# A third Strassen level in five rounds of a two-level product, with loads and small work reordered

## Chip, cores and metric

The kernel runs on one core of a Trainium2 chip. The metric is the device time of that core in microseconds, as a median of three runs. Everything is float32.

The engines named below are TensorE (PE), VectorE (DVE), ScalarE (ACT), GpSimd (POOL) and SyncE (SP), which issues nearly all large transfers.

## The reference

x has the shape 32 x 128 x 2048. It is mixed along its channels with kernels that depend on a condition, passed through a large linear layer with low-rank updates, and added to itself. Then a grouped convolution and a permuted, grouped two-layer network follow, again with a residual.

```python
att = softmax(mlp(cond))                                   # 32 x 8
agg_w = einsum('bk,koi->boi', att, weight)                 # 32 x 128 x 128
h = einsum('boi,bih->boh', agg_w, x) + (att @ bias_k)[:, :, None]
x = x + h @ W.T + bias + sum_e w_e * (h @ A_e.T) @ Bf_e.T  # W: 2048 x 2048, 16 experts
y = conv1d(x, weight9, groups=4) + cond @ c_weight.T + bias
y = y[..., perm] as 16 heads of 128
x = x + unperm(gelu(y @ up_h) @ down_h)                    # 128 -> 512 -> 128
```

The low-rank updates are folded into W ahead of time, and the mixing along channels is applied after the linear layer. So the largest part of the first half is one product of x (all rows, 2048 wide) with a 2048 x 2048 matrix. The change is within that product.

## The kernel before

**Rounds and steps.** The product is cut into 2 x 2 blocks by Strassen-Winograd: seven products of blocks in place of eight. These are the seven rounds, in the order P1, P2, P6, P7, P5, P3, P4 (`ROUNDS`, L48). In each round the weight operand stays and x runs past it in eight steps g = 0 to 7. Step number i is 8 x round + g, so P2 is steps 8 to 15 and P6 is steps 16 to 23. Each step is itself cut by Strassen-Winograd into seven inner products, each of four matmuls of 128x512 (`product` in `multiply`, L347). DVE adds each inner result from its PSUM bank into the round's sums in SBUF (L340).

**The third level.** In the rounds that `THIRD` (L51) names, `multiply_third` (from L408) takes the inner products P2 and P4 of two neighbouring steps together. The even step computes only the five other products (L424) and holds its sums back. The odd step computes its own five, and in between the 28 matmuls of 128x256 (L435) which give P2 and P4 of both steps by one more Strassen-Winograd level. L443 adds these "quarters" into the sums of both steps, L420 the others. The order in the odd step is P1, quarters P1 and P2, P5, quarters P6 and P5, P6, and so on.

The third level needs two kinds of prepared operand, both made on POOL. `third_weights` (L378, operations L386 to L389) makes the weight operands `P_q0` and `P_q1` once a round by 16 operations of 128x256. `third_inputs` (L395, operations L402 to L405) makes the x operand `sq` once a pair by four operations of 128x512, when the x of the odd step is there.

**Preparing operands.** For every step, `x_loads` has SP load one to three tiles of x or of stored sums of x (1 MB each). `x_combine` adds them piece by piece on POOL (L281) and makes four inner combinations (L309 to L312). P6 loads three tiles and has eight piece operations. The next round's weights are loaded and combined in steps 2 to 6 (`outer_weights`; loads on SP, L281 on POOL). `inner_weights` (L251 to L255, 16 operations on POOL) makes the tiles t1, t2 and t4 from them in the last step of the round before. There `third_weights` follows it at once, when the next round has a third level.

**Old sums.** In every round but the first, a step adds to sums that earlier rounds stored in DRAM. `olds_load` has SP load them (`p`, `u` or `c` in the trace, L271), one step ahead. `part_store` writes the new sums out at the end of a step; in a pair, those of both steps at the end of the odd step. `ADDED` lists which sum each round reads and writes. P5 reads and writes two for each step, the other rounds one.

**Slots and queues.** All these tiles share one pool of 24 slots of 1 MB (`SLOTS`, L35). A tile's load or first write waits until the slot's former content has been read for the last time. SP issues its transfers in program order, and stands still at one that waits for its slot. POOL works in program order too.

**Order within a step.** At the top of step i, the code calls x_combine for step i+1 (and `third_inputs` for an even step), x_loads for step i+2, olds_load for step i+1, and in the last step of a round `inner_weights` and `third_weights`. Then the step's products follow. Between them, `between(j)` places other work: the mixing kernels on DVE in rounds P2 to P3 (`mixed_kernel`, L531). At the end of each step, `next(chain)` takes one more part of `small()` (L843), a chain that prepares small things such as att and the tables of the convolution.

From the last round on, the stages of the convolution are mixed in; then follow 128 pairs of `ffn_up` (L803) and `ffn_down` (L814), which the change does not touch.

Of the kernel before, what the change touches and what calls it, by code (L numbers as in the profile page):

```python
# [47 lines left out]
ROUNDS = ("P1", "P2", "P6", "P7", "P5", "P3", "P4")  # L48


THIRD = ("P2", "P7", "P3")  # L51


@with_exitstack
def adaln_ffn_kernel(
# [16 lines left out]
    nc = tc.nc  # L72
# [8 lines left out]
    def slot(name, shape=(P, L)):  # L81
        return big.tile(list(shape), FP, name=name, tag="s")
# [8 lines left out]
    def halves(t):  # L91
        return [t[:, r * NQ : (r + 1) * NQ] for r in range(2)]
# [48 lines left out]
    def a_scale(h, k0, k1):  # L141
        for c in range(2):
            cols = a_sb[h][:, c, :, k0:k1]
            nc.vector.tensor_scalar(cols, cols, wsc[:, c : c + 1], None, ALU.mult)
# [16 lines left out]
    def w_load(kh, oh, kc):  # L161
        t = slot(f"w_{kh}{oh}{kc}", (P, 2, 2, QW))
        nc.sync.dma_start(t.rearrange("p k o c -> p (k o c)"), WT[kh, oh, kc])
        return t
# [99 lines left out]
    def x_load(g, tp, kh):  # L264
        t = slot(f"xt_{g}{tp}{kh}", (P, 2, 2, QW))
        nc.sync.dma_start(t.rearrange("p k s c -> p (k s c)"), xT[g, tp, kh])
        return t

    def part_load(n, g, shape=(P, 2, 2, QW)):
        t = slot(f"{n}_{g}", shape)  # L270
        nc.sync.dma_start(t.rearrange("p k s c -> p (k s c)"), part_d[n, g])  # L271
        return t
# [10 lines left out]
    def x_loads(r, g):  # L283
        return {
            "P1": lambda: [x_load(g, 0, 0)],
            "P2": lambda: [x_load(g, 0, 1)],
            "P6": lambda: [x_load(g, 1, 0), x_load(g, 1, 1), x_load(g, 0, 0)],
            "P7": lambda: [x_load(g, 0, 0), x_load(g, 1, 0)],
            "P5": lambda: [x_load(g, 1, 0), x_load(g, 1, 1)],
            "P4": lambda: [x_load(g, 1, 1)],  # L290
            "P3": lambda: [x_load(g, 0, 1), part_load("s2", g)],
        }[r]()
# [85 lines left out]
    def third_weights(name, rhs):  # L378

        quarters, tt = [], nc.gpsimd.tensor_tensor  # L380
        for i, k in enumerate(("P2", "P4")):
            t = slot(f"{name}_q{i}", (P, 4, 2, NQ))
            q = {"P1": [], "P2": [], "P3": [], "P4": [], "P5": [], "P6": [], "P7": []}
            for kc in range(2):
                (r11, r12), (r21, r22) = (halves(rhs[k][2 * h + kc]) for h in range(2))
                tt(t[:, 0, kc], r12, r11, ALU.subtract)  # L386
                tt(t[:, 1, kc], r22, t[:, 0, kc], ALU.subtract)
                tt(t[:, 2, kc], r22, r12, ALU.subtract)
                tt(t[:, 3, kc], r21, t[:, 1, kc], ALU.subtract)  # L389
                for n, r in zip(q, (r11, r21, r22, t[:, 3, kc], t[:, 0, kc], t[:, 1, kc], t[:, 2, kc])):  # L390
                    q[n].append(r)
            quarters.append(q)
        return quarters

    def third_inputs(i):  # L395

        (x11, x12), (x21, x22) = (
            [xa[n][:, 1, :, h * NQ : (h + 1) * NQ] for h in range(2)] for n in (i, i + 1)
        )
        tt = nc.gpsimd.tensor_tensor  # L400
        t = slot(f"sq_{i}", (P, 4, 2, NQ))
        tt(t[:, 0], x21, x22, ALU.add)  # L402
        tt(t[:, 1], t[:, 0], x11, ALU.subtract)
        tt(t[:, 2], x11, x21, ALU.subtract)
        tt(t[:, 3], x12, t[:, 1], ALU.subtract)  # L405
        return {
            "P1": x11, "P2": x12, "P3": t[:, 3], "P4": x22,
            "P5": t[:, 0], "P6": t[:, 1], "P7": t[:, 2],  # L408
        }
# [568 lines left out]
    steps = [(r, g) for r in ROUNDS for g in range(NG)]  # L978
# [11 lines left out]
    xs = {0: [x_load(0, 0, 0)]}  # L990
# [7 lines left out]
    lhs, sa, tb = {}, {}, {}  # L998
# [17 lines left out]
    rhs = inner_weights("P1", first, make_first)  # L1016
    a_load(1, 0, 4)
    unsummed, unsummed_first = [], list(first)
    olds = {}
    chain = small()  # L1020
    nxt, waiting, ts = {}, {}, {}
    heads = [(g, h) for g in range(NG) for h in range(NH)]

    def olds_load(i):
        r, g = steps[i]
        olds[i] = [old and part_load(old, g) for old, _ in ADDED[r]]

    for i, (r, g) in enumerate(steps):
        ri = i // NG
        last_round = ri + 1 == len(ROUNDS)  # L1030
        if i + 1 < len(steps):
            if i + 1 not in xs:
                xs[i + 1] = x_loads(*steps[i + 1])
            if not last_round:
                lhs[i + 1] = x_combine(*steps[i + 1], xs.pop(i + 1))
                if r in THIRD and g % 2 == 0:
                    sq = third_inputs(i)
        if i + 2 < len(steps) and ri > 0 and not last_round:
            xs[i + 2] = x_loads(*steps[i + 2])
        if i == 0:  # L1040
            olds_load(0)
        if i + 1 < len(steps) and not last_round:
            olds_load(i + 1)
        if g == NG - (1 if ri else 2) and ri < len(ROUNDS) - 1:
            nxt = inner_weights(ROUNDS[ri + 1], [nxt[kc] for kc in range(4)])
            if ROUNDS[ri + 1] in THIRD:
                nxt["quarters"] = third_weights(ROUNDS[ri + 1], nxt)

        if ri == 0:
            ks = blocks[4 + 2 * g : 6 + 2 * g]  # L1050
            if ks:
                two = [wt.pop(k) for k in ks]
                w_make_two(ks, two, sa[ks[0][0]], tb[ks[0][1]])
                made.extend(ks)
                if g == 1:
                    a_scale(1, 0, 4)
                    sa[1] = a_combine(1, nc.gpsimd.tensor_tensor)
                if g == 3:
                    part, tb[0] = b_combine(0, nc.gpsimd.tensor_tensor)
                    for _ in range(4):  # L1060
                        part()
                for k, t in zip(ks, two):
                    unsummed.append((k[1], t))
                    if k[:2] == (1, 0):
                        nxt[k[2]] = t
        elif ri + 1 < len(ROUNDS):
            for k, combine in waiting.items():
                nxt[k] = combine()
            waiting = {}
            if 2 <= g < 6:  # L1070
                waiting[g - 2] = outer_weights(ROUNDS[ri + 1], g - 2)

        if last_round and g == 0:
            late_loads()
        if last_round and g == 2:

            late["te"] = mix.rearrange("p (k r) c -> p k r c", k=2)
            nc.sync.dma_start(mix.rearrange("p k c -> p (k c)"), te_d)
        k0 = 3 * (g - NG)
        if last_round:  # L1080
            stage(k0, stage_first)

        def between(j):
            b = (ri - 1) * (NG - 2) + g
            if ri > 0 and g < NG - 2 and b < B and j < KEXP // 2:
                mixed_kernel(b, (2 * j, 2 * j + 1))
            if ri == 0 and j == 2:
                for k in blocks[6 + 2 * g : 8 + 2 * g]:
                    wt[k] = w_load(*k)
            if ri == 0 and j in (1, 3) and unsummed:  # L1090
                row_sums(*unsummed.pop())
            if ri == 0 and j == 5 and unsummed_first:
                t = unsummed_first.pop(0)
                tt = nc.vector.tensor_tensor
                tt(wsum[:, 0, 0], wsum[:, 0, 0], t[:, 0, 0], ALU.add)
                tt(wsum[:, 0], wsum[:, 0], t[:, 1], ALU.add)
            if last_round:
                if j == 3 and i + 1 < len(steps):
                    lhs[i + 1] = x_combine(*steps[i + 1], xs.pop(i + 1))
                    olds_load(i + 1)  # L1100
                if j in (2, 4):
                    stage(k0 + j // 2, stage_first)
                if j % 2:
                    stage_third(k0 + j // 2)
                else:
                    stage(k0 + j // 2, stage_second)

        if r in THIRD:
            multiply_third(
                r, g, lhs.pop(i), rhs, olds.pop(i), between, rhs["quarters"], sq if g % 2 else None  # L1110
            )
        else:
            multiply(r, g, lhs.pop(i), rhs, olds.pop(i), between)
        xa.pop(i - 1, None)
        next(chain, None)
        if last_round and g >= 6:
            pair(g - 6)
        if last_round and g == 7:
            rings()
            gather_two(0)  # L1120
        if g == NG - 1 and ri + 1 < len(ROUNDS):
            rhs = nxt
            nxt = {}
# [84 lines left out]
```

## Time and profile before

| what | us |
|---|---|
| device time, median of three runs | 2629.53 (2628.84 to 2632.8) |
| device time of the profiled execution | 2631.7 |
| span in the profile of that execution | 2629.9 |
| PE busy in it | 2593.0 (99%) |
| DVE busy | 1407.7 (54%) |
| POOL busy | 1326.1 (50%) |
| ACT busy | 532.6 (20%) |

The profiled execution is 2.2 us above the median and 1.8 us above its own span. Differences worked out from the profile are taken from its own time, and then moved by these 2.2 us.

Busy shares are averages over the whole kernel. The rounds of the product lie within the first half. The costliest groups of all are in the second half and show what PE does there without a pause (line, engine, operation, output<-inputs, shapes, count, busy us, mean ns, idle before):

```profile
L803 PE MATMUL bank<-t,ws 128*128 128x512 f32 x1024 | 460.4, 592 | 1.0 <-DMA ws<-in_ffw 1.0
L814 PE MATMUL bank<-gl,ws 128*128 128x512 f32 x1024 | 460.2, 592 | 0.0
```

For the rounds, the groups of the third level in all its rounds are these, first the four matmuls of an inner product, then DVE's additions, then an ordinary round's matmuls. A float32 matmul leaves two records, of which the mean is given; one of 128x512 takes 0.858 us of the PE in a row of them (3.43 for a product of four), one of 128x256 takes 0.43.

```profile
L424 PE MATMUL bank<-P_t,s_P 128*128 128x512 f32 x384 | 170.7, 592 | 0.0
L420 DVE TENSOR_TENSOR u<-bank,u 128x512 f32<-128x512 f32 x96 | 64.9, 690 | 167.9 <-PE bank L424 150.2
L347 PE MATMUL bank<-P_t,s_P 128*128 128x512 f32 x512 | 225.2, 592 | 0.3 <-POOL P_t L252 0.3
```

In a plain step the 28 matmuls follow each other in 24.03 us; at the third level an even step takes 17.16 and the odd one after it 29.24 or 29.26.

### The profile page before, as it was taken

The numbers are of one execution on the slowest core, as the hardware profiler recorded it, in microseconds if no ns is written. First come the engines' busy times: TensorE is split into PE (matmuls) and PEld (weight loads), VectorE is DVE, ScalarE is ACT, GpSimd is POOL, SyncE is SP. The second block draws the span as 40 slices with busy tenths as digits, with TensorE's granted clock in tenths as the row PEclk, the third lists the DMA queues.
The fourth block names the chain that finished last, engine by engine and source line by source line (L and its number), as shares of the span: only waits on it lengthen the run. The fifth ranks groups of instructions, "written<-read, shape, count | busy, mean of one in ns | idle before, by whom it ended". The sixth has DMA issues, their size and how long they took to land.

```text
span 2629.9 us, 20983 instructions
## 1 busy us (share of the span) xinstructions
PE 2593.0 (99%) x6756; PEld 1283.2 (49%) x6756; DVE 1407.7 (54%) x2238; ACT 532.6 (20%) x1099; POOL 1326.1 (50%) x1110
## 2 busy tenths in 40 slices
PE   9999999799999999999999999999999999999998
PEld 4444455344455544455444445555455545555543
DVE  5554244354354454454366667666666666666610
ACT  0000000000000000000011144444444444444432
POOL 7320845798968743886432334434443344344222
PEclk9999999899999999999999999999999999999999
DMA  8542456678656578566668798777778777777532
GB/s 317 208 168 107 158 236 239 241 305 360 241 202 249 227 292 319 208 239 241 210 217 256 219 320 281 236 228 218 235 241 249 248 218 225 236 250 230 167 122 88
DMA packets 183837, 608.25 MB, mean 231 GB/s; under 512 B 17200, under 2 KB 88368, under 8 KB 139440
## 3 DMA queue, kind: packets, MB, share of 16 engines
q1 hardware_dynamic: 149936, 473.74, 50.8%
q0 software_dynamic: 32992, 132.14, 14.9%
q10 hardware_dynamic: 800, 1.03, 0.1%
q8 instruction: 54, 0.88, 0.1%
q14 instruction: 55, 0.45, 0.1%
HBM read 372.45 MB, written 200.84 MB: 218 GB/s over the span
## 4 chain that ended last, share of the span: by engine, by line
PE 94%; DMA 2%; DVE 2%; POOL 1%; issue 1%; SPq 0%; POOLq 0%; ACT 0%; DVEq 0%; ACTq 0%
PE bank L347 28%; PE bank L803 16%; PE bank L814 16%; PE bank L424 15%; PE bank L659 6%; PE bank L435 5%; PE bank L567 4%; PE bank L222 2%; DMA bf_sb<-in_BfT 1%; DMA p<-p_d 0%; DVE vb L642 0%; DMA ws<-in_ffw 0%; DVE vb L640 0%; POOL wo_P L281 0%; DVE va L641 0%
## 5 line engine op out<-in xcount | busy, mean ns | idle before, releaser
L803 PE MATMUL bank<-t,ws 128*128 128x512 f32 x1024 | 460.4, 592 | 1.0 <-DMA ws<-in_ffw 1.0
L814 PE MATMUL bank<-gl,ws 128*128 128x512 f32 x1024 | 460.2, 592 | 0.0
L821 POOL DMA_INDIRECT out<-t,orow x128 | 151.6, 1184 | 533.3 <-DVE t L819 452.5
L806 ACT ACTIVATE gl<-bank 128x512 f32<-128x512 f32 x512 | 306.0, 598 | 447.2 <-PE bank L803 444.8
L814 PEld LDWEIGHTS bank<-gl,ws 128*128 128x128 f32 x1024 | 194.6, 190 | 233.0 <-issue 231.0
L803 PEld LDWEIGHTS bank<-t,ws 128*128 128x128 f32 x1024 | 194.4, 190 | 227.9 <-issue 222.6
L552 POOL TENSOR_TENSOR x<-x,fb 128x512 f32<-128x512 f32 x128 | 180.8, 1441 | 219.0 <-DMA x<-in_x 172.3
L819 DVE TENSOR_TENSOR t<-bank,t 128x512 f32<-128x512 f32 x128 | 88.4, 691 | 315.4 <-PE bank L814 315.3
L558 ACT ACTIVATE bank<-w,aggb 128x512 f32<-128x512 f32 x128 | 80.8, 684 | 780.1 <-DMA w<-w_d 763.2
L347 PE MATMUL bank<-P_t,s_P 128*128 128x512 f32 x512 | 225.2, 592 | 0.3 <-POOL P_t L252 0.3
L281 POOL TENSOR_TENSOR xt<-xt,xt 128x512 f32<-128x512 f32 x128 | 159.6, 1279 | 98.5 <-DMA xt<-in_xT 64.5
L309 POOL TENSOR_TENSOR s_P<-xt 128x512 f32<-128x512 f32 x56 | 72.1, 1287 | 260.3 <-DMA xt<-in_xT 182.4
L340 DVE TENSOR_TENSOR u<-bank,u 128x512 f32<-128x512 f32 x168 | 110.3, 684 | 165.9 <-PE bank L347 163.4
L531 DVE SCALAR_TENSOR_TENSOR ags<-mix,att_bc,ags 128x128 f32<-128x128 f32 x224 | 178.8, 798 | 4.5
L424 PE MATMUL bank<-P_t,s_P 128*128 128x512 f32 x384 | 170.7, 592 | 0.0
L347 PE MATMUL bank<-wo_P,s_P 128*128 128x512 f32 x384 | 169.1, 592 | 0.9 <-DVE u L340 0.9
L347 PE MATMUL bank<-wo_P,xt 128*128 128x512 f32 x384 | 169.0, 592 | 0.0
L347 PEld LDWEIGHTS bank<-P_t,s_P 128*128 128x128 f32 x512 | 97.2, 190 | 122.3 <-issue 118.6
L787 POOL DMA_INDIRECT t<-hx_d,row x128 | 130.9, 1023 | 50.1 <-issue 25.6
L420 DVE TENSOR_TENSOR u<-bank,u 128x512 f32<-128x512 f32 x96 | 64.9, 690 | 167.9 <-PE bank L424 150.2
L659 PE MATMUL bank<-va,tw_l 128*128 128x256 f32 x512 | 122.4, 380 | 1.9 <-DVE va L643 1.8
L659 PEld LDWEIGHTS bank<-va,tw_l 128*128 128x128 f32 x512 | 96.6, 190 | 44.6 <-issue 34.2
(187 smaller groups left out, 3453.2 us busy)
## 6 DMA issues: line engine op xcount, KB each, us to landing
xt<-in_xT SPq DMA_DIRECT2D x88, 1024.0 KB, 9.0
u<-u_d SPq DMA_DIRECT2D x40, 1024.0 KB, 11.4
wo_P<-wb_d SPq DMA_DIRECT2D x36, 1024.0 KB, 12.0
u<-c_d SPq DMA_DIRECT2D x64, 512.0 KB, 7.4
x<-in_x SPq DMA_DIRECT2D x32, 1024.0 KB, 8.4
xg<-x SPq DMA_DIRECT2D x256, 128.0 KB, 5.2
hx_d<-x1t SPq DMA_DIRECT2D x32, 1024.0 KB, 5.9
hx_d<-ht SPq DMA_DIRECT2D x32, 1024.0 KB, 7.1
```

The source lines that it names most:

```text
L281: nc.gpsimd.tensor_tensor(out[:, i, j], a[:, i, j], b[:, i, j], op)
L347: nc.tensor.matmul(ps, lhsT=lhs[k][:, bass.ts(kc, P)], rhs=rhs[k][kc], start=first and kc == 0, stop=last and kc == 3, skip_group_check=True,)
L424: nc.tensor.matmul(ps, lhsT=lhs[k][:, bass.ts(kc, P)], rhs=rhs[k][kc], start=first and kc == 0, stop=last and kc == 3, skip_group_check=True,)
L435: nc.tensor.matmul(out, lhsT=sq[k][:, i, bass.ts(kc, P)], rhs=quarters[i][k][kc], start=first and i == 0 and kc == 0, stop=last and i == 1 ...
L531: nc.vector.scalar_tensor_tensor(ag, mix[:, k], att, ag, ALU.mult, ALU.add)
L552: nc.gpsimd.tensor_tensor(xt[:, f], xt[:, f], late["fb"][:, f], ALU.add)
L659: nc.tensor.matmul(out, lhsT=w[:, 2 * i + r], rhs=rhs, start=first and r == 0, stop=last and r == 1, skip_group_check=True,)
L787: nc.gpsimd.indirect_dma_start(out=t.rearrange("p k t -> p (k t)"), out_offset=None, in_=hx_d[g].rearrange("l k t -> l (k t)"), in_offset= ...
L803: nc.tensor.matmul(pu, lhsT=w[:, m * P : (m + 1) * P], rhs=t[:, 0], start=True, stop=True)
L806: nc.scalar.activation(gl[m], pu, AF.Gelu)
L814: nc.tensor.matmul(pd, lhsT=w[:, (MC + m) * P : (MC + m + 1) * P], rhs=gl[m], start=(m == 0), stop=(m == MC - 1),)
L821: nc.gpsimd.indirect_dma_start(out=out, out_offset=bass.IndirectOffsetOnAxis(ap=orow[:, g, h : h + 1], axis=0), in_=t[:, 1], in_offset=None,)
```

## The change

Five rounds get the third level in place of three: P2, P6, P7, P5 and P3. In P2, P6 and P5 the last pair (steps g = 6 and 7) stays at two levels (`SKIP`, `in_pair`). This makes 17 pairs in place of 12.

`third_weights` is no longer called in the last step of the round before, but in the first step of the round itself, after the x_combine of the second step and after `third_inputs`. In P6, `third_inputs` runs on DVE, after the even step's products; in the other rounds it stays on POOL.

On SP's queue, `olds_load` for step i+1 now comes before x_loads for step i+2. For steps of P6, x_loads is called from `between(3)` within the step, so after other transfers of the same step's top. From step 6 on, `next(chain)` is called twice in a step.

```diff
--- before.py
+++ after.py
@@ -48,7 +48,8 @@
 ROUNDS = ("P1", "P2", "P6", "P7", "P5", "P3", "P4")
 
 
-THIRD = ("P2", "P7", "P3")
+THIRD = ("P2", "P6", "P7", "P5", "P3")
+SKIP = (("P2", 3), ("P6", 3), ("P5", 3))
 
 
 @with_exitstack
@@ -392,12 +393,15 @@
             quarters.append(q)
         return quarters
 
-    def third_inputs(i):
+    def in_pair(r, g):
+        return r in THIRD and (r, g // 2) not in SKIP
+
+    def third_inputs(i, eng):
 
         (x11, x12), (x21, x22) = (
             [xa[n][:, 1, :, h * NQ : (h + 1) * NQ] for h in range(2)] for n in (i, i + 1)
         )
-        tt = nc.gpsimd.tensor_tensor
+        tt = eng.tensor_tensor
         t = slot(f"sq_{i}", (P, 4, 2, NQ))
         tt(t[:, 0], x21, x22, ALU.add)
         tt(t[:, 1], t[:, 0], x11, ALU.subtract)
@@ -1033,18 +1037,19 @@
                 xs[i + 1] = x_loads(*steps[i + 1])
             if not last_round:
                 lhs[i + 1] = x_combine(*steps[i + 1], xs.pop(i + 1))
-                if r in THIRD and g % 2 == 0:
-                    sq = third_inputs(i)
-        if i + 2 < len(steps) and ri > 0 and not last_round:
-            xs[i + 2] = x_loads(*steps[i + 2])
+                if in_pair(r, g) and g % 2 == 0 and r != "P6":
+                    sq = third_inputs(i, nc.gpsimd)
         if i == 0:
             olds_load(0)
         if i + 1 < len(steps) and not last_round:
             olds_load(i + 1)
+        ahead = i + 2 < len(steps) and ri > 0 and not last_round
+        if ahead and steps[i + 2][0] != "P6":
+            xs[i + 2] = x_loads(*steps[i + 2])
         if g == NG - (1 if ri else 2) and ri < len(ROUNDS) - 1:
             nxt = inner_weights(ROUNDS[ri + 1], [nxt[kc] for kc in range(4)])
-            if ROUNDS[ri + 1] in THIRD:
-                nxt["quarters"] = third_weights(ROUNDS[ri + 1], nxt)
+        if r in THIRD and g == 0:
+            quarters = third_weights(r, rhs)
 
         if ri == 0:
             ks = blocks[4 + 2 * g : 6 + 2 * g]
@@ -1087,6 +1092,8 @@
             if ri == 0 and j == 2:
                 for k in blocks[6 + 2 * g : 8 + 2 * g]:
                     wt[k] = w_load(*k)
+            if j == 3 and ahead and steps[i + 2][0] == "P6":
+                xs[i + 2] = x_loads(*steps[i + 2])
             if ri == 0 and j in (1, 3) and unsummed:
                 row_sums(*unsummed.pop())
             if ri == 0 and j == 5 and unsummed_first:
@@ -1105,14 +1112,18 @@
                 else:
                     stage(k0 + j // 2, stage_second)
 
-        if r in THIRD:
+        if in_pair(r, g):
             multiply_third(
-                r, g, lhs.pop(i), rhs, olds.pop(i), between, rhs["quarters"], sq if g % 2 else None
+                r, g, lhs.pop(i), rhs, olds.pop(i), between, quarters, sq if g % 2 else None
             )
         else:
             multiply(r, g, lhs.pop(i), rhs, olds.pop(i), between)
         xa.pop(i - 1, None)
+        if in_pair(r, g) and g % 2 == 0 and r == "P6":
+            sq = third_inputs(i, nc.vector)
         next(chain, None)
+        if i > 5:
+            next(chain, None)
         if last_round and g >= 6:
             pair(g - 6)
         if last_round and g == 7:
```

## The prediction

> **What bounds the kernel now.** I read the page's forty slices first. PE is at 9 in all slices but one, where the granted clock dips too. So the kernel is bound by TensorE, and a change can pay only by fewer matmuls, or by closing that hole at about 490 us.
>
> ```profile
> PE   9999999799999999999999999999999999999998
> PEclk9999999899999999999999999999999999999999
> ```
>
> The list of PE's waits (us in total, times, longest) says that the hole is one wait; everything else together is some 10 us.
>
> ```profile
> PE bank L435 <- DVE p L443: 18.9, 1, 18.9
> PE bank L222 <- DVE w L225: 1.9, 3, 1.1
> ```
>
> Next, windows cut at the first matmul of the rounds P2, P6, P7, P5, P3 (length; busy us of PE, PEld, DVE, ACT, POOL; clock; DMA share; GB/s). P7 and P3 take 185.7, which is PE alone; P5, a round without the third level, 192.3. P2 loses its 18.9. POOL is the next busiest engine, 93% in P6.
>
> ```profile
> 305.80:511.80 206.00, 187.14 (x545) 104.13 (x544) 83.91 (x128) 2.36 (x4) 119.83 (x100) 0.96 0.62 238
> 511.80:704.80 193.00, 192.69 (x450) 85.19 (x449) 87.60 (x107) 0.63 (x1) 179.67 (x151) 1.00 0.76 298
> 704.80:890.50 185.70, 185.70 (x546) 103.38 (x545) 87.38 (x123) 0.00 (x0) 135.44 (x114) 1.00 0.61 238
> 890.50:1082.80 192.30, 192.30 (x449) 85.14 (x449) 101.18 (x161) 0.00 (x0) 108.70 (x88) 1.00 0.69 273
> 1082.80:1268.40 185.60, 185.60 (x545) 103.30 (x544) 87.83 (x124) 0.00 (x0) 142.18 (x122) 1.00 0.56 221
> ```
>
> Then the chain of waits around the hole (start, us, what). SP issues all big loads in program order and stands still until a slot is free. POOL's weight combination (wo_P) frees a slot at 476.5; only then can SP issue the last x load of P6, and behind it the old sum p of P2's last step, which takes 12.44 us to land.
>
> ```profile
> 466.72 4.96 POOL wo_P L281 x5
> 472.80 3.71 POOL wo_P L281 x3
> ...
> 476.95 0.38 SPq L266
> ...
> 477.43 12.44 DMA p<-p_d
> ```
>
> PE's timeline shows the price: 18.86 us idle, then a group of 16 that takes 5.07 instead of the 3.45 of its sisters. The hole costs 18.86 + 1.62 = 20.5 us.
>
> ```profile
> 491.43 5.07 PE L435 MATMUL bank<-P_q,sq 128*128 128x256 f32 x16 [18.86 <-DVE p L443]
> ```
>
> [...] Here a 128x512 addition takes 1.27 us on POOL, 0.69 on DVE: a ratio of 1.85. [...]
>
> **The change, part by part.**
>
> *Third level in P6 and P5, not in the last pairs of P2, P6, P5.* A pair has 8 products of 4 matmuls less by the third level: two plain steps take 2 x 24.03 = 48.06 us; a pair at the third level 17.16 (even) + 29.24 (odd) = 46.40. Gain 1.66. Pairs go from 12 to 17 (P2 -1, P6 +3, P5 +3): 5 x 1.66 = 8.3 us.
>
> *Old sums ahead of x.* The old sum of step 15 leaves SP in front of P6's x loads. By the slots freed before it, it is issued at about 447 and lands by 459, against about 472.5 when PE needs its result. The hole goes: -20.5. P6 also took 0.7 above 8 x 24.03 = 192.3 in before, the start of its first step waiting for P_t of L252 and what surrounds it; -0.7. So without new waits the five rounds take 187.3 + 187.3 + 185.6 + 187.3 + 185.6 = 933.1 against 962.6: -29.5.
>
> *third_weights at g == 0 of its own round.* This is the part with a price. The 16 POOL operations of 128x256 at 0.72 take 11.5 us; they stood at the end of the round before, and now stand behind the x_combine of the round's second step (10.3; 15.9 in P6) and third_inputs (5.0). The deadline: the first odd step reads quarter 1's t[1] of kc 1 in its second block. In P3 of before that is 17.17 (even step) + 10.32 + 3 x 0.43 = 28.78 us after the round's first matmul. The operation that makes it is the 14th of 16 and ends 10.1 after third_weights starts. By round:
>
> P5, the worst. Its inner weights need for t2 the slot that P7's sq of the last pair holds. POOL's timeline (start, us, operation, idle before):
>
> ```profile
> 878.53 1.27 POOL L251 TENSOR_TENSOR P_t<-wo_P 128x512 f32<-128x512 f32 x1 [7.99 <-PE bank L424]
> 882.04 1.27 POOL L252 TENSOR_TENSOR P_t<-wo_P,P_t 128x512 f32<-128x512 f32 x1 [2.25 <-PE bank L435]
> ...
> 896.36 5.05 POOL L255 TENSOR_TENSOR wo_P<-wo_P 128x512 f32<-128x512 f32 x4
> 901.36 5.10 POOL L281 TENSOR_TENSOR xt<-xt,xt 128x512 f32<-128x512 f32 x4
> ...
> 911.66 4.94 POOL L281 TENSOR_TENSOR xt<-xt,xt 128x512 f32<-128x512 f32 x4
> ```
>
> P7's last step starts at 861.07, so t2 starts 21.0 after it; inner weights end 19.3 later (901.4); x_combine 10.3; third_inputs 5.0; 10.1 to the operation: 65.7. The deadline is 29.26 (that step) + 28.78 = 58.04. PE waits 7.7. It comes in four pieces of under 3 us, as kc by kc and quarter by quarter gets ready, with a 0.43 matmul between, so I take 0.6 for the clock, not 1.6. Range 5 to 10; the later pairs of P5 lose nothing, since the weights are made once a round.
>
> P2: its second step's x lands at 314.7 in before; combined and third_inputs done at 325.0; +10.1 = 335.1 against 305.80 + 28.78 = 334.6: 0.6 (0 to 2). P6: the third x of its first step needs a slot that the stores of step 13 free (landed at 456.1), so it lies ready at about 459; x_combine 15.9, inner weights 20.6, the second x_combine 15.9 (third_inputs is off POOL) and 10.1: 521.5, against 305.8 + 187.3 + 0.6 + 28.78 = 522.5. One us of slack in a chain of four links, so I take 0.3 (0 to 3). P7: about 3 us of slack, 0 (0 to 4). P3: t4's slot waits for P5's last reads, 10.4 into P5's last step: 29.8 against 28.78: 1.1 (0 to 3). Sum 7.7 + 0.6 + 0.6 + 0.3 + 1.1 = 10.3.
>
> *third_inputs of P6 on DVE.* Three times four operations, 0.69 each by DVE's row: 2.8 us, against 5.1 on POOL. [...] DVE is busy 87.6 of 193 in P6. Behind it stand only additions whose banks are waited for later. Nothing, at worst 1 us a pair [...]. Below nothing it can't go: what POOL saves is counted in P6's deadline.
>
> *P6's x half a step later.* The loads only change places with others on SP, which issues as soon as a slot is free: behind the two or four loads of old sums, about 2.5 us each when queued. In P6 x still lies 7 to 20 us ahead of its combination. Nothing, but for the first step, counted above.
>
> *Chain twice as dense.* The same instructions, at about step 11 instead of 17 at the end; on PE they are a few small matmuls. Nothing; up to 1.
>
> *More DVE adds in P5.* P5 adds into two accumulators, so a pair has DVE busy about 41 of 46.4 us, with mixed_kernel between. Bank order keeps PE ahead: nothing, up to 1 a pair.
>
> Sum: -29.5 + 10.3 = -19.2. The profiled execution took 2631.7 (span 2629.9): 2612.5. It lies 2.2 above the median, so 2610.3.
>
> **Rivals.**
> A, no new wait: POOL gets t2's slot earlier or x_combine starts earlier, so P5's deadline holds. For: the tiles' places are by the pool. Against: before itself shows the 2.25 us wait for that slot. 2631.7 - 29.5 - 2.2 = 2600; with small waits 2601.
> B, more waits of the same kind: P6, P7 and P3 miss their deadlines by 2 to 4 each, because an x load or a store behind other transfers on SP frees a slot later; 5 to 12 more, 2615 to 2622, about 2619. For: their slack is 1 to 3 us. Against: it is counted with before's own durations.
> C, slower: POOL becomes the bound of P6. It was busy 179.7 there; P7's third_weights leave (-11.5), its own come (+11.5), and the round shrinks to 187.3, so 7.6 us are spare. Each step's x comes half a step later; if POOL stands idle for it more than 4 us a step, 8 x 4 = 32 less 7.6 is 24.4: that eats the gain of 19.2 and 5.3 more. At 4.5 us a step: 36 - 7.6 = 28.4, so 2639. It decides from 4 us a step. Against: the 7 to 20 us of lead.
> D, the hole stays since SP is held elsewhere ahead of the old sum: +20.5, so 2631, no change.
>
> **How the numbers follow.** Main case 0.62 (2606 to 2615), A 0.13, B 0.17, C 0.06, D 0.02. The range from 2601 to 2619 takes the main case, most of A and half of B: about 0.8. A measurement tells about 0.2%, 5.3 us, from no change. Faster 0.92 (main, A, B); same 0.02 (D); slower 0.06 (C).
>
> **What would show it.** Right: no wait of L435 for the p of L443, the clock's 8 gone; PE waiting 6 to 9 us for P_q in the first odd step of P5; round windows near 188, 188, 186, 196, 187. Wrong on P5: no P_q wait there. Wrong on the pairs: matmul pitch unlike 46.4. Wrong on P6: POOL at over 95% with waits of PE for s_P.

## The result and the profile after

The changed kernel takes 2629.09 us (median of 12 runs, 2627.48 to 2631.21) against 2631.52 us for the kernel before, also in 12 runs. The ratio is 0.9994, with a 95% interval of 0.9985 to 1.0002: no change. The forecast was 2610.3 us, with a range from 2601 to 2619.

The profiled execution took 2628.8 us, 2.9 less than that of before. The page's slices, PE busy and granted clock, show that the hole at 490 us is gone:

```profile
PE   9999999999999999999999999999999999999998
PEclk9999999999999999999999999999999999999999
```

In its place the list of PE's waits has a new first line. L439 and L388 of the changed kernel are L435 and L387 of before (quarters' matmuls, second operation of `third_weights`):

```profile
PE bank L439 <- POOL P_q L388: 17.2, 12, 2.2
PE bank L223 <- DVE w L226: 3.1, 3, 2.3
```

17.2 us in twelve waits of at most 2.2 are no hole that a slice can show. Windows cut at the first matmul of P2, P6, P7, P5 and P3 show where they lie (length; busy us of PE, PEld, DVE, ACT, POOL; clock; DMA share; GB/s):

```profile
305.66:493.87 188.21, 187.59 (x522) 98.72 (x521) 87.61 (x124) 3.00 (x5) 137.72 (x120) 1.00 0.70 269
493.87:682.61 188.74, 187.59 (x522) 98.72 (x521) 96.85 (x131) 0.00 (x0) 164.85 (x142) 1.00 0.77 295
682.61:876.42 193.81, 188.81 (x545) 104.78 (x544) 90.43 (x123) 0.00 (x0) 149.37 (x129) 0.98 0.58 228
876.42:1073.31 196.89, 190.57 (x521) 99.88 (x520) 124.75 (x190) 0.00 (x0) 128.46 (x111) 0.98 0.69 267
1073.31:1266.15 192.84, 188.75 (x546) 104.55 (x545) 92.81 (x124) 0.00 (x0) 148.25 (x126) 0.98 0.54 213
```

P2 and P6 lost 17.8 and 4.3 us, as forecast within 1.2. P7, P5 and P3 grew by 8.1, 4.6 and 7.2. In sum the five rounds went from 962.6 to 960.5 us. By the working of the forecast, PE without any new wait would need 187.3, 187.3, 185.6, 187.3 and 185.6 for them, 933.1. So the waits and their slow clock cost 0.9, 1.4, 8.2, 9.6 and 7.2, which makes 27.3; 10.3 were forecast.

All of it lies at one place in each round, the first odd step. This is PE in P7 (start, us, operation, idle before):

```profile
710.09 0.59 PE L439 MATMUL bank<-P_q,sq 128*128 128x256 f32 x2
711.31 0.70 PE L439 MATMUL bank<-P_q,sq 128*128 128x256 f32 x2 [0.62 <-POOL P_q L388]
714.25 0.70 PE L439 MATMUL bank<-P_q,sq 128*128 128x256 f32 x2 [2.25 <-POOL P_q L388]
717.09 4.63 PE L439 MATMUL bank<-P_q,sq 128*128 128x256 f32 x10 [2.14 <-POOL P_q L388]
```

The last matmul of quarter P6 starts at 717.09; in a round without waits it would start 28.78 us after the round's first matmul, at 711.39. So POOL is 5.7 us late. After that, ten records take until 721.52, which is 4.43 us, where ten take 2.16 in a row at a granted clock of 1.00. From 717.09 to 721.52 the granted clock was 0.50. That costs 2.3 more, and the next group, at 0.96, 0.2 (3.59 to the group after it, in place of 3.43).

POOL's timeline leads from there to the cause:

```profile
640.26 9.83 POOL L282 TENSOR_TENSOR xt<-xt,xt 128x512 f32<-128x512 f32 x8 [7.53 <-DMA xt<-in_xT]
...
670.91 1.27 POOL L252 TENSOR_TENSOR P_t<-wo_P 128x512 f32<-128x512 f32 x1
...
706.88 0.72 POOL L387 TENSOR_TENSOR P_q<-wo_P 128x256 f32<-128x256 f32 x1
...
716.32 0.72 POOL L388 TENSOR_TENSOR P_q<-P_t,P_q 128x256 f32<-128x256 f32 x1
```

From 640.26 on POOL works with no pause above 0.3 us: x_combine, a weight combination, x_combine, `inner_weights` from 670.91, x_combine, `third_inputs`, `third_weights`. From the start of `inner_weights` to the operation that PE waits for are 20.6 + 10.3 + 5.1 + 10.1 = 46.1 us. PE needs it 28.78 after the round's start. So **POOL must start `inner_weights` 17.3 us ahead of the round.** In P7 it starts 11.7 ahead (670.91 against 682.61); in the kernel before it was 26.0 (678.76 against 704.80):

```profile
678.76 1.26 POOL L251 TENSOR_TENSOR P_t<-wo_P 128x512 f32<-128x512 f32 x1
```

PE came 22.2 us earlier, and POOL only 7.9. POOL lost 7.53 us at 640.26 alone, where it waited for x.

In P3 the same sum gives 12.0 ahead (1061.27 against 1073.31), and there too POOL had waited before, for the stored sum s of x:

```profile
1051.23 4.93 POOL L282 TENSOR_TENSOR xt<-xt,s 128x512 f32<-128x512 f32 x4 [14.98 <-DMA s<-s_d]
...
1061.27 1.26 POOL L252 TENSOR_TENSOR P_t<-wo_P 128x512 f32<-128x512 f32 x1
...
1106.63 0.72 POOL L388 TENSOR_TENSOR P_q<-P_t,P_q 128x256 f32<-128x256 f32 x1
```

### The profile page after: what moved, and what is told of

The parts are those of the page before. It is cut to its first block, busy times and chain, and to the rows that moved or that the text cites. A ratio compares the mean times of both kernels' runs of the same rounds, so it can differ in the third digit from the quotient of the medians.

```text
span 2627.0 us, 21296 instructions
## 1 busy us (share of the span) xinstructions
PE 2591.4 (99%) x6876; PEld 1307.7 (50%) x6876; DVE 1449.3 (55%) x2290; ACT 533.2 (20%) x1099; POOL 1356.6 (52%) x1150
## 4 chain that ended last, share of the span: by engine, by line
PE 84%; POOL 9%; DMA 4%; DVE 2%; issue 1%; SPq 0%; POOLq 0%; ACT 0%; DVEq 0%; ACTq 0%
PE bank L428 17%; PE bank L807 17%; PE bank L818 16%; PE bank L348 14%; PE bank L439 7%; PE bank L663 6%; PE bank L571 4%; PE bank L223 2%; POOL xt L282 2%; DMA xt<-in_xT 1%; DMA bf_sb<-in_BfT 1%; POOL P_t L253 1%; POOL wo_P L256 1%; POOL P_t L252 1%; POOL P_t L254 1%
## 5 line engine op out<-in xcount | busy, mean ns | idle before, releaser
L556 POOL TENSOR_TENSOR x<-x,fb 128x512 f32<-128x512 f32 x128 | 175.4, 1399 | 213.2 <-DMA x<-in_x 151.6
L424 DVE TENSOR_TENSOR u<-bank,u 128x512 f32<-128x512 f32 x168 | 110.7, 687 | 193.8 <-PE bank L428 173.8
L428 PE MATMUL bank<-wo_P,s_P 128*128 128x512 f32 x448 | 199.1, 592 | 0.0
L310 POOL TENSOR_TENSOR s_P<-xt 128x512 f32<-128x512 f32 x56 | 72.8, 1300 | 239.3 <-DMA xt<-in_xT 187.3
L535 DVE SCALAR_TENSOR_TENSOR ags<-mix,att_bc,ags 128x128 f32<-128x128 f32 x224 | 190.8, 852 | 4.5
L428 PEld LDWEIGHTS bank<-P_t,s_P 128*128 128x128 f32 x544 | 103.7, 191 | 115.7 <-issue 112.2
L428 PEld LDWEIGHTS bank<-wo_P,s_P 128*128 128x128 f32 x448 | 85.1, 190 | 95.2 <-issue 92.6
L439 PE MATMUL bank<-P_q,sq 128*128 128x256 f32 x408 | 103.3, 401 | 17.2 <-POOL P_q L388 17.2
```

Of the source, the lines that this page charges most:

```text
L428: nc.tensor.matmul(ps, lhsT=lhs[k][:, bass.ts(kc, P)], rhs=rhs[k][kc], start=first and kc == 0, stop=last and kc == 3, skip_group_check=True,)
L439: nc.tensor.matmul(out, lhsT=sq[k][:, i, bass.ts(kc, P)], rhs=quarters[i][k][kc], start=first and i == 0 and kc == 0, stop=last and i == 1 ...
L535: nc.vector.scalar_tensor_tensor(ag, mix[:, k], att, ag, ALU.mult, ALU.add)
L556: nc.gpsimd.tensor_tensor(xt[:, f], xt[:, f], late["fb"][:, f], ALU.add)
```

## The experiments

The theory from these traces was that POOL's chain, with its x, is too long for the first odd step in P7, P5 and P3 once PE comes earlier. The rivals were the place of `third_weights` as such, the x of P6 half a step later, and the order of the loads on SP.

| run | edit to the changed kernel | us | ratio to before |
|---|---|---|---|
| the changed kernel | | 2629.1 | 0.9994 (0.9985 to 1.0002) |
| e1_weights_back | third_weights at its old place | 2628.7 | 0.9991 (0.9982 to 1.0) |
| e2_order_only | kernel before, old sums first | 2629.0 | 0.9994 (0.9985 to 1.0003) |
| e3_skip_first | first pairs plain, not last | 2607.1 | 0.9915 (0.9898 to 0.9931) |
| e4_inputs_dve | first third_inputs on DVE | 2615.0 | 0.9938 (0.9922 to 0.9955) |
| e5_x_early | P6's x at its old place | 2629.6 | 0.9997 (0.9988 to 1.0005) |
| e6_x_first | x before old sums but in P6 | 2621.8 | 0.996 (0.9946 to 0.9974) |
| e8_order_skip | kernel before, old sums first, P2's last pair plain | 2610.8 | 0.9922 (0.9905 to 0.9939) |
| e9_weights_dve | first third_inputs and third_weights on DVE | 2670.4 | 1.015 (1.0133 to 1.0166) |
| e10_p6_plain | P6 at two levels | 2624.3 | 0.9977 (0.9966 to 0.9987) |
| e11_first_but_p3 | first pairs plain but P3's, x first | 2624.5 | 0.9976 (0.9966 to 0.9987) |
| e12_skip_two | only P7's and P5's first pairs plain, x first | 2632.2 | 1.0005 (0.9996 to 1.0013) |
| e13_p7_last | P7's last pair plain too | 2629.1 | 0.9991 (0.9984 to 0.9997) |

### The place of third_weights (e1_weights_back)

```diff
             nxt = inner_weights(ROUNDS[ri + 1], [nxt[kc] for kc in range(4)])
-        if r in THIRD and g == 0:
-            quarters = third_weights(r, rhs)
+            if ROUNDS[ri + 1] in THIRD:
+                nxt["quarters"] = third_weights(ROUNDS[ri + 1], nxt)
```

> The changed kernel with third_weights back in the last step of the round before, ahead of x_combine and third_inputs. Theory of the position (the later place of third_weights costs the waits of P7, P5 and P3, 8.2 + 9.6 + 7.2 = 25 us): about 2604 us. Theory of the chain (POOL has the same work to do before the first odd step's quarter P6, whichever part comes first: x_combine 10.3, third_inputs' first half 2.6 and all of third_weights 11.5 are 24.4 against 25.4 now): only 1 us a round less, 2624 to 2628, and PE then waits for sq in place of P_q.

2628.7 us: the chain, not the place. PE waits for something else at nearly the same point, the x of the odd step, which x_combine now makes 11.5 us later:

```profile
PE bank L428 <- POOL xt L282: 18.0, 4, 6.7
```

I had named sq as the last to come; it was x itself, some 10 us earlier in the step. The price is the same, since POOL's sum of work ahead of the first odd step is the same.

### Which steps pay (e3_skip_first)

```diff
-SKIP = (("P2", 3), ("P6", 3), ("P5", 3))
+SKIP = (("P2", 0), ("P6", 0), ("P7", 0), ("P5", 0), ("P3", 0))
```

> The changed kernel, but the first pair of every one of the five rounds stays at two levels, in place of the last pair of three: 15 pairs. If the lost time lies only in the first odd step of each round: 2629.1 - 27.4 + 2 x 1.67 = 2605 us and no wait for P_q. If POOL falls behind for good within P6 (its loads of x), the waits only come later: above 2612.

2607.1 us. With two pairs less than the changed kernel, it is 22 us faster, and nothing of the new waits is left. In these rounds the list has this as its longest:

```profile
PE bank L428 <- POOL s_P L310: 0.8, 1, 0.8
```

So the loss is all in the first odd steps, and no later step waits for POOL by more than this.

### POOL's 5.1 us (e4_inputs_dve)

```diff
-                if in_pair(r, g) and g % 2 == 0 and r != "P6":
+                if in_pair(r, g) and g % 2 == 0 and r != "P6" and (g or r == "P2"):
                     sq = third_inputs(i, nc.gpsimd)
...
-        if in_pair(r, g) and g % 2 == 0 and r == "P6":
+        if in_pair(r, g) and g % 2 == 0 and (r == "P6" or (g == 0 and r != "P2")):
             sq = third_inputs(i, nc.vector)
```

> The changed kernel with third_inputs of the first pair of P7, P5 and P3 on DVE too. Theory of the chain: POOL reaches third_weights 5.1 us earlier in each, so the delays go from 5.6, 7.7 and about 5 us to 0.5, 2.6 and 0, and 2609 us come out (2606 to 2613). If DVE is late with them behind mixed_kernel[...]: less than half of that, above 2619.

2615.0: 14 us less, of 20 expected; it lies between the two expected ranges. P7 is 2.8 us late (713.33 against 681.75 + 28.78) and P5 4.5 (905.09 against 871.80 + 28.78); 0.5 and 2.6 were expected. Two things made the difference. One is that POOL's `third_weights` now runs beside DVE's `third_inputs`; its first four operations take over 1 us in place of 0.72, so that the fourteenth ends 11.9 us after the start, not 10.1:

```profile
701.36 1.17 POOL L387 TENSOR_TENSOR P_q<-wo_P 128x256 f32<-128x256 f32 x1
702.61 1.05 POOL L388 TENSOR_TENSOR P_q<-wo_P,P_q 128x256 f32<-128x256 f32 x1
```

The other is that PE is slow after its waits, as in the changed kernel, where the granted clock was 0.50 in that stretch of P7. PE's groups of ten after the last wait in P7, P5 and P3:

```profile
713.33 3.89 PE L439 MATMUL bank<-P_q,sq 128*128 128x256 f32 x10 [2.24 <-POOL P_q L388]
...
905.09 4.63 PE L439 MATMUL bank<-P_q,sq 128*128 128x256 f32 x10 [2.24 <-POOL P_q L388]
...
1096.78 2.42 PE L439 MATMUL bank<-P_q,sq 128*128 128x256 f32 x10 [1.25 <-POOL P_q L388]
```

In P7 a single wait of 2.24 us makes the group 3.89 long in place of 2.42 (P6 of the changed kernel, after a wait of 1.15); three waits of 5.0 in all made it 4.63 in the changed kernel. In P3, after 1.25 us of waiting, it takes 2.42. So here the loss does not follow the waiting time in proportion: 2.24 us of waiting cost 1.5, 5.0 cost 2.2, and 1.25 nothing more than the 1.15 there.

### P6's x half a step later, and the order on SP (e5_x_early, e6_x_first)

```diff
-        if ahead and steps[i + 2][0] != "P6":
+        if ahead:
             xs[i + 2] = x_loads(*steps[i + 2])
...
-            if j == 3 and ahead and steps[i + 2][0] == "P6":
-                xs[i + 2] = x_loads(*steps[i + 2])
```

> The changed kernel with P6's loads of x at the top of the step again, after the old sums but ahead of the next weights. Theory of the later x (P7's 8.2 us come from POOL's 7.5 us wait for the x of P6's last step, which stood behind the weights on SP): P7's wait shrinks to under 2 us, 2621 to 2625. Theory of the slots (POOL frees the slots that SP needs, so the order on SP only moves the wait): P7 stays within 2 us of its 193.8, 2627 to 2631. The hole of P2 does not come back in either.

2629.6. P7 takes from 683.46 to 877.29, which is 193.83, as if nothing had been changed. POOL now waits 9.81 us for the x of P7's first step instead of 7.53 for that of P6's last. So the place of these loads on SP here only chose which x was late, and the half step later is not the cause.

In e6_x_first the three lines with `x_loads` for other rounds stand above those with `olds_load` again.

> The changed kernel with x_loads ahead of the old sums again, in all rounds but P6, whose x stay half a step later. If P3's 7.2 us come from its first stored sum landing behind two old sums on the same engines (2.5 us each, so 5 us): P3 at 186 to 188, all in all 2622 to 2625. If SP waits for slots there anyway: unchanged, 2628 to 2631. The hole of P2 does not come back, since P6's x still stand behind the old sum.

2621.8, 7.3 less, and P3 takes 185.68 us (1076.20 to 1261.88), its time without a wait. POOL gets the first stored sum of P3 at 1045.93, 30.3 us ahead of the round; in the changed kernel it was 22.1 (1051.23 against 1073.31):

```profile
1045.93 4.95 POOL L282 TENSOR_TENSOR xt<-xt,s 128x512 f32<-128x512 f32 x4 [15.86 <-DMA s<-s_d]
```

It needs 17.3 + 10.1 for x_combine, so 27.4. This is the cause in P3: the old sums, moved ahead of x in P2's favour, delay x at the end of P5, a round that reads two old sums a step. In the changed kernel from 1036 to 1048, behind the issues of the old sums, x and s, the transfers ran at 418 GB/s with the DMA busy throughout (share 1.01), which is 2.5 us for 1 MB.

### What the hole was worth by itself (e2_order_only, e8_order_skip)

e2_order_only is the kernel before with the two blocks at the top of the step exchanged, olds_load first.

> The kernel before with nothing but the old sums' loads moved ahead of x's. Theory of the hole (its 20.5 us were the whole price): 2611 us, with P7 and P3 still at 185.7. Theory of the chain (the hole also gave POOL time; P7 had 9.9 us to spare before, and P3 0.8): the first odd step of P7 is up to 10 us late, so 2615 to 2622, with waits in P7 or P3.

Both expectations missed. 2629.0 came out, and the waits were neither in P7 nor in P3. They stayed at the end of P2:

```profile
478.63 6.70 PE L435 MATMUL bank<-P_q,sq 128*128 128x256 f32 x16 [5.48 <-DVE p L443]
...
511.52 1.61 PE L347 MATMUL bank<-P_t,s_P 128*128 128x512 f32 x2 [2.83 <-POOL P_t L252]
515.42 2.08 PE L347 MATMUL bank<-P_t,s_P 128*128 128x512 f32 x2 [2.29 <-POOL P_t L252]
```

The old sum is still 5.5 us late: SP issued it only at 472.3, when POOL's weight combination had freed a slot. Then P6's `inner_weights` come late. PE is slow after both: 6.70 us for a group of 16 that takes 3.62 elsewhere, 1.61 and 2.08 for two records that take 1.02, and the granted clock from 480 to 500 was 0.88. e8_order_skip also takes the third level from P2's last pair:

```diff
-                if r in THIRD and g % 2 == 0:
+                if r in THIRD and g % 2 == 0 and (r, g) != ("P2", 6):
                     sq = third_inputs(i)
...
-        if r in THIRD:
+        if r in THIRD and (r, g // 2) != ("P2", 3):
             multiply_third(
```

> The kernel before with the old sums ahead of x, and P2's last pair at two levels; no third level in P6 and P5, third_weights at its old place. The order alone gave 2 us, with waits for the old sum and then for P6's weights (P_t) at the same place. If the skipped pair is the other half of the cure (POOL's 5.1 us of third_inputs, and slots): no wait at the end of P2, 2631 - 20.5 + 1.7 = 2612, if P7 and P3 keep their deadlines. If POOL's lateness was hidden by the hole in any case: above 2618.

2610.8, with no wait in the five rounds; SP issues the old sum at 447.0. So the order alone does not close the hole, and the order with the skipped pair does; the skipped pair alone was not tried. With both, P7 and P3 keep their deadlines although PE comes 19 us earlier. This version has 11 pairs. The changed kernel, with 17, is 18 us slower: **its third level in P6 and P5, and what came with it, took back 18 of the 20 us that closing the hole gave.**

### P7: pairs in P6 (e10_p6_plain)

```diff
-THIRD = ("P2", "P6", "P7", "P5", "P3")
+THIRD = ("P2", "P7", "P5", "P3")
```

> The changed kernel with P6 at two levels. Theory of the slots (pairs in P6 hold sq, held sums and stored sums, so SP gets slots for x only when POOL frees them, POOL waits for x, and is 5.6 us late at P7's first odd step): no wait in P7; 2629.1 - 8.2 - 1.4 + 3 x 1.67 = 2624.5 us. Theory of the hole alone (POOL is late in P7 because PE comes 20 us earlier, whatever P6 does): P7 keeps its 8, and about 2633 come out.

2624.3; 2624.5 were expected. P7 takes 185.68 us (684.97 to 870.65), and only P5 and P3 wait:

```profile
PE bank L439 <- POOL P_q L388: 10.0, 6, 2.2
```

POOL starts P7's `inner_weights` 19.2 us ahead of the round, where it needs 17.3 and had 11.7 in the changed kernel:

```profile
665.77 1.26 POOL L252 TENSOR_TENSOR P_t<-wo_P 128x512 f32<-128x512 f32 x1
```

PE comes 2.4 us later, and POOL 5.1 earlier. So P7's 8.2 us come from P6's third level. What in it delays POOL stays open. The slots are one candidate, and SP's issues in the changed kernel fit: it issued the x of step 23 at 632.8, when POOL's weight combination (ended 632.7) had freed the slot, and POOL then waited until 640.1 for it. The other is POOL's own work: this run also drops P6's `third_weights`. From P6's `inner_weights` to P7's, POOL is busy 158.2 of 191.3 us, in the changed kernel 171.4 of 195.4; so it has 13 us less work and is idle 9 us longer. The two were not tried apart, nor were the tiles of the pairs one by one.

### P5: the slot of t2 (e13_p7_last)

```diff
-SKIP = (("P2", 3), ("P6", 3), ("P5", 3))
+SKIP = (("P2", 3), ("P6", 3), ("P7", 3), ("P5", 3))
```

> The changed kernel with P7's last pair at two levels too: 16 pairs, and no sq of that pair in the slot that P5's t2 needs. Theory of the slot: POOL then starts P5's inner weights when the x of P5's first step has landed and is combined, at about 863.7 in place of 868.1, against a deadline 1.67 later; P5's first odd step is some 2 to 3 us late in place of 7.7, and with less of the slow clock 2624 us come out (2622 to 2626). If the slot is not what holds it: P5 keeps its 9.6, and 2631 come out.

2629.1 us, the median over 20 runs (2621.7 to 2632.81, more spread than others): that of the changed kernel, and outside what the theory of the slot gave. Its mechanism is there all the same. In the changed kernel POOL waited 2.25 us for PE ahead of t2; here it starts `inner_weights` at 864.87 and goes on without that wait:

```profile
868.14 1.26 POOL L253 TENSOR_TENSOR P_t<-wo_P,P_t 128x512 f32<-128x512 f32 x1 [2.25 <-PE bank L439]
```

```profile
864.87 1.27 POOL L252 TENSOR_TENSOR P_t<-wo_P 128x512 f32<-128x512 f32 x1
```

PE's delay falls to 3.9 us (911.14 against 878.50 + 28.78), from 7.8. The half that is left is not due to t2's slot: POOL had waited 11.3 us for the x of P5's first step, until 854.85, and so starts `inner_weights` 13.6 us ahead of the round, not 17.3. And PE, slow after the wait, takes a part of the gain back:

```profile
908.20 0.70 PE L439 MATMUL bank<-P_q,sq 128*128 128x256 f32 x2 [1.19 <-POOL P_q L388]
911.14 4.64 PE L439 MATMUL bank<-P_q,sq 128*128 128x256 f32 x10 [2.24 <-POOL P_q L388]
915.57 4.07 PE L428 MATMUL bank<-P_t,s_P 128*128 128x512 f32 x8
```

4.43 us to the next group in place of 2.16, and 3.91 in place of 3.43: 2.8 us lost so, where the changed kernel lost 1.8 at a granted clock of 0.57. P5 takes 193.93, 3.0 less, and P7 with its pair given up 195.69, 1.9 more. This leaves a gain of 1.1 us in the two rounds, less than the spread of the runs.

### third_weights on DVE (e9_weights_dve)

```diff
-        if r in THIRD and g == 0:
-            quarters = third_weights(r, rhs)
+        if r in ("P2", "P6") and g == 0:
+            quarters = third_weights(r, rhs, nc.gpsimd)
...
+            if r in ("P7", "P5", "P3") and g == 0 and j == 2:
+                late["q"] = third_weights(r, rhs, nc.vector)
```

with `third_inputs` as in e4_inputs_dve.

> The changed kernel with third_weights of P7, P5 and P3, and third_inputs of their first pairs, on DVE. Theory of the chain: what POOL still does ends before the deadlines, so the 25 us of P7, P5 and P3 go: 2604 us (2601 to 2608), without waits of L439 in these rounds. If DVE is late with 9.6 us more work in the even step[...]: waits for P_q or sq remain, 2608 to 2618.

2670.4 us, outside both. PE waits 20 us for DVE in each of the three rounds (60.4 in all). DVE's timeline, and POOL's beside it:

```profile
696.19 0.41 DVE L387 TENSOR_TENSOR P_q<-wo_P 128x256 f32<-128x256 f32 x1
696.70 1.32 DVE L388 TENSOR_TENSOR P_q<-wo_P,P_q 128x256 f32<-128x256 f32 x1
697.94 1.48 DVE L389 TENSOR_TENSOR P_q<-wo_P,wo_P 128x256 f32<-128x256 f32 x1
```

```profile
691.04 5.08 POOL L282 TENSOR_TENSOR xt<-xt,xt 128x512 f32<-128x512 f32 x4
696.20 1.53 POOL L310 TENSOR_TENSOR s_P<-xt 128x512 f32<-128x512 f32 x1
```

The first addition began in a gap of 0.08 us between two of POOL's (696.12 to 696.20) and took 0.41 us. The others ran beside POOL's x_combine and took 1.3 to 1.5; the same operation, L387, takes 1.48 at 700.76. So the 16 take 21.5 us, and the additions that free PE's banks stand behind them.

### Keeping more pairs (e11_first_but_p3, e12_skip_two)

```diff
-SKIP = (("P2", 3), ("P6", 3), ("P5", 3))
+SKIP = (("P2", 0), ("P6", 0), ("P7", 0), ("P5", 0))
```

This is e11_first_but_p3; e12_skip_two has `SKIP = (("P7", 0), ("P5", 0))`. Both have x first as in e6_x_first.

> The changed kernel with the first pair in place of the last at two levels in P2, P6, P7 and P5, P3 whole, and x_loads ahead of the old sums except in P6: 16 pairs. If the first odd steps were the only price, and the order on SP that of P3: no wait left above 1 us, 2607.1 - 1.7 = 2605 us (2603 to 2608). If P3 or P2 is late again: 2609 to 2613.

2624.5, a miss. P3 waits 8.2 us for P_q again, as P5's last pair now has the third level ahead of P3's first. And with x first, P6's last pair waits for its old sum, 4.8 us at 669.03, as P2's last pair did in the kernel before.

> As the one before, but only the first pairs of P7 and P5 at two levels: 18 pairs. P2's and P6's first pairs give 1.67 each and cost 0.9 and 1.4: 2604 us. If P2's last pair with its third level takes POOL's time and slots from P6's weights again, as in the run with the order alone: waits at the end of P2, above 2612.

2632.2. The waits foreseen at the end of P2 came one round later: POOL is late in P6's and P3's first odd steps (nearly all of 14.8 us of waits for P_q), and P6's last pair waits 3.5 us for its old sum. So a third level on both sides of a round's border costs more than a pair gives, at P2/P6 and at P5/P3. e3_skip_first stays the fastest.

## Why the prediction was wrong

- *The hole goes, -20.5.* Right in size: e8_order_skip took 20 us off. The issue at about 447 came true as well (447.7 in the changed kernel). But the prediction put it down to the order on SP, and the order alone leaves it at 472.3 and gives 2 us (e2_order_only); the skipped pair had its part.
- *Five more pairs, -8.3.* Right. e3_skip_first and e10_p6_plain are where 1.67 a pair puts them, within some 2 us. The words "8 products of 4 matmuls less" do not fit the sum: in a pair, 16 matmuls of 128x512 give way to 28 of 128x256, which is the work of 14.
- *P5 waits 7.7.* Right: the operation ended at 912.95, the deadline was 905.2, and t2 started 21.0 after P7's last step began. e13_p7_last confirms the slot, but behind it stands a wait that was not counted: with the slot free, 3.9 us of delay are left, as the x of P5's first step comes late too.
- *P7: "about 3 us of slack, 0 (0 to 4)".* **This step failed.** It was 5.7 late, 8.2 us with the clock. The prediction shows no sum for these 3 us. POOL started P7's `inner_weights` 11.7 us ahead of the round and needed 17.3. Its start hangs on a loop: SP waits for slots that POOL frees, POOL for the x that SP loads. P6's third level is what makes POOL late (e10_p6_plain: 19.2 ahead without it, and no wait); whether by slots or by POOL's added work is open. "In P6 x still lies 7 to 20 us ahead" was wrong: POOL waited for x in several steps, up to 7.5 us. The trace of before showed such waits already, three of 2.0 to 2.7 us in P6, this one among them:

```profile
645.66 9.93 POOL L281 TENSOR_TENSOR xt<-xt,xt 128x512 f32<-128x512 f32 x8 [2.70 <-DMA xt<-in_xT]
```

- *P3: 1.1.* **This failed too**: 5.3 late, 7.2 with the clock. The step looked at t4's slot. What came last was the stored sum of x behind two old sums (e6_x_first). The prediction had put the new order on SP at no cost in any round.
- *0.6 for the clock, as the waits come in pieces.* An estimate that no trace of before had shown, and mis-sized: about 6 us in three rounds (2.5, 1.8 and 1.9). The pieces were of 0.2 to 2.25 us, with one matmul of 0.70 to 1.22 between them. In the ten records after the last piece, the granted clock was 0.50 in P7, 0.57 in P5 and 0.56 in P3; after the single hole of before it was 0.72 (491.43 to 496.33).
- *P2 0.6 and P6 0.3.* 0.9 and 1.4: right in place, small. (By their own figures the terms of P2 and P3 are 0.5 and 1.0.)
- *third_inputs of P6 on DVE: at worst 1 us a pair.* An estimate; it showed no wait of its own. But the four operations took 0.87 to 1.21 us in P6's first pair, beside POOL; in its other two pairs, with POOL idle, they took 0.68 to 0.69. e4_inputs_dve and e9_weights_dve show what more of them do. The trace of before held a price for such work, in the mixing kernels, which also have all their tiles in SBUF: L531 takes 0.35 us in the median where no POOL addition runs, and 1.24 where it lies wholly beside POOL's additions.
- *P6's x half a step later: nothing.* Right (e5_x_early).
- *Chain twice as dense.* No wait came from it; it was not tried alone.
- *More DVE adds in P5: nothing.* Right: PE waited for no bank of DVE there. DVE was busy 124.8 of P5's 196.9 us, less than the 41 of 46.4 that were reckoned.

Rival B was nearest, with late first pairs in P7 and P3, but it gave the extra waits 5 to 12 us, and they came to 17. The sum was -29.5 + 10.3; the waits were 27.3.

## What to carry to other kernels

A stall of the bounding engine can also be slack for the engines that feed it. Before its length is booked as gain, compute for each later deadline how far ahead the feeding engine must start, and recount its lead with the stall gone and its new work in place; here it needed 17.3 us and had 11.7. An order of transfers that cures one round should be tried in that round alone: here it brought P3's x late (7.2 us, gone in e6_x_first). And work that is moved to DVE beside a busy POOL has to be priced at the speed measured there (for L531 in before, 1.24 us in place of 0.35).

## What was not expected of the hardware

- DVE's additions with both inputs in SBUF slowed 3.4 times beside POOL's in e9_weights_dve (from 0.41 us, which the one that began in POOL's gap took, to 1.4 from one start to the next), and POOL's own rose from 1.27 to about 1.44. The additions with one input from PSUM did not slow: L424 of the changed kernel takes 0.69 us in the median, beside POOL's additions or not.
- PE slowed after waits that were short one by one (in P7 of the changed kernel none was above 2.25 us, and the granted clock fell to 0.50). After single waits of 1.25 us (e4_inputs_dve) and 1.63 (e5_x_early), ten records took 2.42 and 2.43 us, as after one of 0.62 in P2 of the changed kernel (2.43). After a single one of 2.24 us they took 1.5 more, after three of 5.0 in all 2.2 more. Beyond that the length did not decide: in groups of 16 that take 3.62 us elsewhere, the wait of 5.48 us in e2_order_only cost 3.1 (6.70) and that of 18.86 in the kernel before 1.5 (5.07). The forecast's 1.62 for the latter set 5.07 against 3.45, which is the time from such a group's start to the next group's.
